# Message loop of a four-layer graph network: the older tile's product matmuls stand ahead of the next tile's source matmuls on TensorE

## The chip, the cores and the metric

The kernel runs on one core of a Trainium2 chip. The metric is the device time in microseconds, median of three runs. The profile is one further execution of the same program on the chip, taken by the hardware profiler.

## The reference

2708 nodes with 128 features each and a sparse adjacency matrix (about 8 edges in a row of 2708, each row divided by its count) go through four layers. Each layer normalises the rows, takes a relu and adds its result to x. The change concerns layer 1 and the product of layer 2 that is made beside it:

```python
# layer 1
s = node_feats @ msg_w[:, :D].T
d = node_feats @ msg_w[:, D:].T
messages = gelu(s[:, None, :] + d[None, :, :] + msg_b)
aggregated = einsum('ijd,ij->id', messages, adj)
combined = concatenate([node_feats, aggregated], axis=-1)
h = gelu(combined @ upd_w.T + upd_b) + node_feats
x = x + (h - mean(h)) / sqrt(var(h) + LN_EPS) * ln_w + ln_b
# layer 2
h = relu(layernorm(x))
x = x + relu(adj @ (h @ w2))
```

Layer 0 is a hyperbolic layer with one product by adj, layer 3 has one more product by adj, and neither is touched.

## The kernel before, in words

The 2708 rows are 22 tiles of 128 (the last has 20 rows). In a first stage (to about 222 us) the kernel reads adj transposed, keeps a mask of its nonzeros in 8-bit floats, finds for every row the columns of its edges, and runs layer 0. It also writes the rows d to a table in HBM (`d_hbm`).

Layer 1 is the message loop (L1734 to L1876). It makes the messages of existing edges only. For each tile t, `messages` (L1749) does this:

- GpSimd (POOL) issues seven indirect gathers from `d_hbm` (L1727): four into `g` (edges 3 to 6 of each row) and three into `gt` (the remaining edges, 384 to a tile). The last tile has two, both into `gt`. Each of the two buffers exists four times. The first two edges of each row, `early`, have been gathered before the loop.
- `sources(t)` (L1734 to L1747): for `gt` the s of the row that an edge belongs to is needed. Nine matmuls of TensorE (three chunks of 128 edges, three bf16 parts of s each) write it to a PSUM tile `msg`. Two such PSUM tiles exist (the other six banks hold the running product), and the matmuls `own` of the prelude use the same two.
- VectorE (DVE) adds s to `early` and `g` (L1773) and `msg` to `gt` (L1776); ScalarE (ACT) takes the gelus (L1781, L1782).
- TensorE sums the messages by row into a free part of the same `msg` tile: six matmuls on `early` and `g` (L1787) and three on `gt` with a 0/1 matrix `rt` (L1789), which the profile counts as 12 and 6, two passes each.
- ACT copies the sums to `aggs` (L1801), TensorE multiplies them by the update weights into `msg` (L1803), DVE reads that (L1804), ACT takes the gelu (L1807), and DVE adds h (L1808).

After every two tiles `update` (L1814) normalises them: DVE forms the mean (L1613), ACT squares (L1616), DVE makes a root out of nine small operations (L1604, L770 to L779, L1620), ACT scales (L1819), DVE multiplies and adds to x (L1826, L1829). The same follows for x (`jx`, `nmx`), then ACT takes the relu (L1626) and makes, with DVE (L1631, L1633), three bf16 parts of layer 2's h in `parts`. These parts go over the parts of s, which `sources` of that tile has used up.

Layer 2's product adj @ h runs in the same loop. `add_products(accs, parts, s)` (L1641) has 18 matmuls for a tile s: three parts by six blocks of columns, 512 columns each but the last (148). In tile t of the loop it takes s = t - 4 (`LAG`), called `share`, where 4 <= t < 20. The shares 16 to 19 follow after the loop (L1874 to L1876), and those of tiles 20 and 21 are in the next stage.

In 9 of the tiles from 5 to 16 DVE also compares a row tile of adj with the row's value (L1661, two halves of 1354 columns), which SyncE's queue loads. For the first tiles a prelude (L1700) makes v and tmp for four later tiles at a time.

The order on each engine is set by a scheduler that is part of the language. `queue_behind(ins)` (L763) adds one condition: what is issued inside it stands behind `ins` in its own engine's list. In `messages` these conditions give TensorE's order: the sums of tile t, then the sources of t + 1 (behind the last sum, `done`), then the product share, then the update matmul of tile t, and the sums of tile t + 1 behind that one (`sum_after`). Apart from such conditions and the data, the scheduler orders DVE and ACT itself, so their lists can differ where only TensorE's conditions do.

Of the kernel before, what the change touches and what calls it, by code (L numbers as in the profile page):

```python
# [543 lines left out]
@with_exitstack  # L544
def gnn_stack_kernel(ctx: ExitStack, tc: tile.TileContext, *args: bass.AP):
    nc = tc.nc
    N = args[0].shape[0]
    flag = ctx.enter_context(tc.tile_pool(name="flag", bufs=1)).tile([1, 1], I32, name="flag")
    with ExitStack() as sparse:
        sparse_stack(sparse, tc, flag, *args)  # L550
    failed = nc.values_load(flag[0:1, 0:1], min_val=0, max_val=1)
    with tc.If(failed > 0):
        with ExitStack() as dense:
            dense_stack(dense, tc, *args)


def sparse_stack(
# [21 lines left out]
    nc = tc.nc  # L579
    N = x_in.shape[0]  # L580
    T = -(-N // P)
# [6 lines left out]
    def rows(t):  # L588
        return min(P, N - t * P)
# [5 lines left out]
    def chunks(t):  # L595

        return NQ if rows(t) == P else tails(t) + 1
# [3 lines left out]
    def cols(t0, t1):  # L601
        return slice(t0 * P, min(t1 * P, N))
# [160 lines left out]
    def queue_behind(ins):  # L763
        return ExitStack() if ins is None else tc.issue_after(ins.ins)
# [31 lines left out]
    with ExitStack() as st:  # L796
# [142 lines left out]
        latest = {}  # L939
# [700 lines left out]
    def add_products(accs, parts, t, which=None):  # L1640

        for k in range(3):
            for b in range(len(blocks)) if which is None else which:
                sl = cols(*blocks[b])
                last = nc.tensor.matmul(  # L1645
                    accs[b][:, : sl.stop - sl.start],
                    parts[:, t, k, :],
                    mask[:, t, sl],
                    start=(t == 0 and k == 0),
                    stop=(t == T - 1 and k == 2),  # L1650
                )
        return last
# [41 lines left out]
    with ExitStack() as st_m:  # L1694
# [30 lines left out]
        def gather(g, table, n):  # L1725
            for q in range(g.shape[1]):
                nc.gpsimd.indirect_dma_start(  # L1727
                    out=g[:n, q, :],
                    out_offset=None,
                    in_=d_hbm,  # L1730
                    in_offset=bass.IndirectOffsetOnAxis(ap=table[:n, q : q + 1], axis=0),
                )

        def sources(t, after):  # L1734

            ps = ps_one.tile([P, BANK], F32, tag="one", name=f"msg{t}")
            for q in range(chunks(t)):
                for k in range(3):
                    with queue_behind(after):
                        nc.tensor.matmul(  # L1740
                            ps[:, q * D : (q + 1) * D],
                            r_all[:, t, q * P : (q + 1) * P],
                            parts[:, t, k, :],
                            start=(k == 0),
                            stop=(k == 2),
                        )
            return ps  # L1747

        def messages(t, ps, u, total, add_after, sum_after, share):  # L1749


            n = rows(t)
            nq = chunks(t)
            own_places = n == P
            if own_places:
                ge = early_d[t // EACH][:, t % EACH, :, :]
                g = gath_p.tile([P, HEAD - EARLY, D], F32, tag="g", name=f"g{t}")
                gather(g, head_c[:, t, :], n)
            gt = gath_p.tile([P, nq, D], F32, tag="gt", name=f"gt{t}")
            gather(gt, tail_c[:, t, :], P)  # L1760
            rt = hot_p.tile([P, nq, P], F32, tag="rt", name=f"rt{t}")
            with queue_behind(first):
                nc.vector.tensor_tensor(
                    rt,
                    col_i.unsqueeze(1).to_broadcast([P, nq, P]),
                    tail_r[:, t, :nq].unsqueeze(2).to_broadcast([P, nq, P]),
                    ALU.is_equal,
                )

            ahead = rows_done[t - 2] if t >= 2 else (None, None)  # L1770
            with queue_behind(add_after), queue_behind(ahead[0]):
                for a in (ge, g) if own_places else ():
                    nc.vector.tensor_add(  # L1773
                        a, a, v[:, t, :].unsqueeze(1).to_broadcast([P, a.shape[1], D])
                    )
                last = nc.vector.tensor_add(  # L1776
                    gt, gt, ps[:, : nq * D].rearrange("p (q d) -> p q d", d=D)
                )
            with queue_behind(ahead[1]):
                for a in (ge, g) if own_places else ():  # L1780
                    nc.scalar.activation(a, a, AF.Gelu)  # L1781
                nc.scalar.activation(gt, gt, AF.Gelu)  # L1782
            sums = ps[:, NQ * D : NQ * D + P]
            with queue_behind(sum_after):
                for q in range(HEAD if own_places else 0):
                    part = ge[:, q, :] if q < EARLY else g[:, q - EARLY, :]
                    nc.tensor.matmul(sums, part, ident, start=(q == 0), stop=False)  # L1787
                for q in range(nq):
                    done = nc.tensor.matmul(  # L1789
                        sums,  # L1790
                        gt[:, q, :],
                        rt[:, q, :],
                        start=(not own_places and q == 0),
                        stop=(q == nq - 1),
                    )
            next_ps = sources(t + 1, done) if t + 1 < T else None
            if share is not None:
                with queue_behind(done):
                    done = add_products(accs, parts, share)
            agg = small.tile([P, P], F32, tag="agg", name=f"aggs{t}")  # L1800
            nc.scalar.copy(agg, sums)  # L1801
            with queue_behind(done):
                new = nc.tensor.matmul(ps[:, :D], agg, upd_w[:, 1, :], start=True, stop=True)  # L1803
            nc.vector.scalar_tensor_tensor(  # L1804
                u, ps[:, :D], val[:, t : t + 1], tmp[:, t, :], op0=ALU.mult, op1=ALU.add
            )
            curved = nc.scalar.activation(u, u, AF.Gelu)  # L1807
            added = nc.vector.scalar_tensor_tensor(  # L1808
                u, u, 1.0, h[:, t, :], op0=ALU.mult, op1=ALU.add, accum_out=total
            )  # L1810
            rows_done.append((added, curved))
            return last, next_ps, new
# [31 lines left out]
        first = prelude(0)  # L1844
        begun = 1
        ps = sources(0, None)

        last_two = max(0, T - 2)
        starts = list(range(0, last_two, 2)) + list(range(last_two, T))
        for t0, t1 in zip(starts, starts[1:] + [T]):  # L1850
            n = t1 - t0
            u = small.tile([P, n, D], F32, tag="u", name=f"u{t0}")
            total = group_p.tile([P, n], F32, tag="total", name=f"totu{t0}")
            for k in range(n):
                t = t0 + k

                share = t - LAG if LAG <= t < T - 2 else None
                last, ps, new = messages(
                    t, ps, u[:, k, :], total[:, k : k + 1], last_check, new, share
                )  # L1860
                if begun < len(groups):
                    prelude(begun)
                    begun += 1
                elif t % 4 != 3 and t < T - 5 and unchecked:

                    with queue_behind(last):
                        last_check = compare(
                            unchecked.pop(0),
                            lambda k: hT[:, k * middle : (k + 1) * middle],
                            junk_p,  # L1870
                            [(0, middle), (middle, N)],
                        )
            update(t0, n, u, total)
# [183 lines left out]
```

## Time and profile before

| what | us |
|---|---|
| median of 3 runs (lowest 555.25, highest 558.63) | 555.48 |
| the profiled execution | 556.43 |
| its span | 554.6 |
| PE busy | 422.5 (76%) |
| DVE busy | 419.9 (76%) |
| ACT busy | 236.6 (43%) |
| POOL busy | 234.7 (42%) |
| mean granted TensorE clock | 0.892 of full speed |

The message loop lies between 222 and 423 us of the span. A view by stage gives busy time there: in 361.5 to 413.4 (51.9 us) PE 41.92, DVE 36.05, ACT 23.79, POOL 39.64; in 413.4 to 423.4 (10 us) PE 5.28, DVE 5.50, ACT 5.34, POOL 0.00; in 423.4 to 442.0 (18.6 us) PE 18.60, DVE 11.34.

How such lines are read: a group or a piece of the timeline begins with start and length in us, then engine, line and operation, out<-in with shapes, and how many instructions it merges. The bracket holds the idle time of the engine just before, and what ended it. A line of the waits view has the waiting engine and line, what it waited for, and the total in us, the number of waits and the longest. Waits of POOL of 0.3 us are the time between two issues and no real waits. PE matmuls overlap, so a piece of the timeline can end after the next begins.

### The profile page before, as it was taken

How to read it: one execution, taken by the hardware profiler on the slowest of the kernel's cores; microseconds unless marked ns; L12 is line 12 of the kernel's file. 1: busy time of each engine (PE TensorE's matmuls, PEld its weight loads, DVE VectorE, ACT ScalarE, POOL GpSimd, SP SyncE). 2: the span in 40 equal slices, each digit the busy share in tenths (PEclk: the TensorE clock that was granted, in tenths of full speed). 3: DMA queues.
4: the chain of work that ended last, by engine and by line, in shares of the span. 5: the costliest groups of instructions: out<-in, count | busy, mean ns of one | idle time of the engine just before them, and what ended most of it. 6: DMA issues, size and time to landing. Idle time of an engine off the chain costs nothing.

```text
span 554.6 us, 8223 instructions
## 1 busy us (share of the span) xinstructions
PE 422.5 (76%) x2504; PEld 262.1 (47%) x2504; DVE 419.9 (76%) x1743; ACT 236.6 (43%) x570; POOL 234.7 (42%) x268
## 2 busy tenths in 40 slices
PE   0981999999993062276877968879877999989994
PEld 0760354464753051265646644646553555445652
DVE  6977986767998989437679786879546599998742
ACT  2867966766424131324535434454534344300100
POOL 8800022220047777777777777777760000000000
PEclk9996899999998555668888987989997999999998
DMA  8893779970031132123146473752220250399011
GB/s 260 278 318 124 227 248 331 305 210 2 1 115 43 52 96 52 48 52 104 51 151 203 153 206 101 232 170 52 54 47 2 83 219 1 116 390 394 20 57 51
DMA packets 39332, 77.89 MB, mean 140 GB/s; under 512 B 5754, under 2 KB 18614, under 8 KB 37722
## 3 DMA queue, kind: packets, MB, share of 16 engines
q1 hardware_dynamic: 30270, 63.15, 33.1%
q0 software_dynamic: 7264, 13.40, 9.6%
q10 hardware_dynamic: 1744, 0.72, 0.5%
q8 instruction: 22, 0.36, 0.3%
q14 instruction: 32, 0.26, 0.1%
HBM read 73.63 MB, written 3.62 MB: 139 GB/s over the span
## 4 chain that ended last, share of the span: by engine, by line
PE 37%; DVE 31%; DMA 12%; POOL 6%; issue 6%; ACT 5%; ACTq 0%; DVEq 0%
PE three L1645 8%; PE acc L1324 8%; PE two L1645 7%; DMA gt<-d_hbm,tail_c 5%; DMA a<-in_adj_t_dram 4%; POOL g L1727 4%; DVE eq L1661 3%; POOL gt L1727 3%; PE msg L1787 3%; DMA layer_w<-in_L_gnn_layer_dram 2%; PE d L948 1%; DMA hT<-in_adj_dram 1%; PE pk L1028 1%; DVE mask L994 1%; PE neigh L1684 1%
## 5 line engine op out<-in xcount | busy, mean ns | idle before, releaser
L1645 PEld LDWEIGHTS <-parts 128*128 128x128 bf16 x792 | 75.3, 101 | 90.4 <-issue 9.5
L1645 PE MATMUL two<-mask,parts 128*128 128x512 fp8e4 (+1 forms) x396 | 88.8, 381 | 9.3 <-ACT parts L1630 5.1
L1727 POOL DMA_INDIRECT g<-d_hbm,head_c x84 | 82.9, 986 | 25.8 <-issue 22.6
L1324 PE MATMUL acc<-mask,parts 128*128 128x512 fp8e4 (+1 forms) x396 | 79.6, 355 | 0.7 <-DVE parts L786 0.4
L1645 PE MATMUL three<-mask,parts 128*128 128x512 fp8e4 (+1 forms) x396 | 79.0, 354 | 0.6 <-ACT parts L1630 0.5
L1727 POOL DMA_INDIRECT gt<-d_hbm,tail_c x65 | 62.7, 964 | 19.8 <-issue 15.2
L1120 POOL DMA_INDIRECT val<-in_adj_dram,ai x22 | 22.0, 998 | 104.5 <-DVE left L1108 91.3
L1324 PEld LDWEIGHTS <-parts 128*128 128x128 bf16 x396 | 36.6, 98 | 47.6 <-ACT parts L783 7.5
L1523 POOL DMA_INDIRECT early<-d_early,early_c x42 | 43.0, 1023 | 12.8 <-issue 11.9
L999 ACT ACTIVATE mask<-a 128x2048 fp8e4<-128x2048 uint32 (+3 forms) x27 | 38.2, 1434 | 10.0 <-DMA a<-in_adj_t_dram 9.8
L1661 DVE TENSOR_SCALAR_CACHE_REDUCE eq<-row,val 128x2708 fp8e4<-128x2708 f32 (+1 forms) x13 | 39.4, 3031 | 2.4 <-DMA row<-in_adj_dram 2.3
L1028 PE MATMUL pk<-mask,shifts 128*128 128x512 fp8e4 (+1 forms) x132 | 31.1, 372 | 13.0 <-ACT mask L999 12.4
L1740 PE MATMUL msg<-parts,r_all 128*128 128x128 bf16 x195 | 15.7, 227 | 19.0 <-DVE u L1804 13.7
L1661 DVE TENSOR_SCALAR_CACHE_REDUCE eq<-hT,val 128x1354 fp8e4<-128x1354 f32 x18 | 29.1, 1619 | 0.1
L1787 PE MATMUL msg<-ident,early 128*128 128x128 f32 x84 | 16.4, 327 | 16.6 <-DVE gt L1776 13.3
L1776 DVE TENSOR_TENSOR gt<-gt,msg 128x384 f32<-128x384 f32 (+1 forms) x22 | 12.0, 545 | 21.5 <-DMA gt<-d_hbm,tail_c 19.1
L1710 PE MATMUL own<-pair_w,hT 128*128 128x256 f32 x44 | 15.9, 503 | 13.6 <-ACT exs L1268 9.6
L1787 PE MATMUL msg<-ident,g 128*128 128x128 f32 x168 | 25.5, 302 | 0.0
L926 ACT ACTIVATE h<-x,n_nb,n_rstd 128x128 f32<-128x128 f32 x44 | 18.2, 486 | 17.0 <-DVE n_nb L920 17.0
L1787 PEld LDWEIGHTS msg<-ident,g 128*128 128x128 f32 x168 | 24.2, 221 | 0.2
L1740 PEld LDWEIGHTS <-r_all 128*128 128x128 fp8e4 x195 | 13.5, 102 | 22.1 <-issue 18.0
L1773 DVE TENSOR_TENSOR g<-g,v 128x512 f32<-128x512 f32 x21 | 14.5, 689 | 11.3 <-DMA g<-d_hbm,head_c 11.3
(407 smaller groups left out, 867.2 us busy)
## 6 DMA issues: line engine op xcount, KB each, us to landing
a<-in_adj_t_dram SPq DMA_DIRECT2D x25, 1024.0 KB, 7.6
row<-in_adj_dram SPq DMA_DIRECT2D x12, 1354.0 KB, 9.6
hT<-in_adj_dram SPq DMA_DIRECT2D x18, 677.0 KB, 4.1
a<-in_adj_t_dram SPq DMA_DIRECT2D x5, 296.0 KB, 4.9
g<-d_hbm,head_c POOLq DMA_INDIRECT x84
a<-in_adj_t_dram SPq DMA_DIRECT2D x5, 256.0 KB
d_hbm<-v SPq DMA_DIRECT2D x5, 256.0 KB, 3.7
out_dram<-x SPq DMA_DIRECT2D x5, 256.0 KB
```

The source lines that it names most:

```text
L926: nc.scalar.activation(h[:, t, :], x[:, t, :], AF.Relu, bias=node("nb")[:, t : t + 1], scale=node("rstd")[:, t : t + 1],)
L999: nc.scalar.activation(mask[:, g : g + n, sl], bits[:, :n, :w], AF.Sign, saturate=False)
L1028: nc.tensor.matmul(pk[:, :w], shifts[:, t, :], mask[:, t, sl], start=(t == 0), stop=(t == T - 1))
L1120: nc.gpsimd.indirect_dma_start(out=val[:, t : t + 1], out_offset=None, in_=flat, in_offset=bass.IndirectOffsetOnAxis(ap=ai[:, t : t + 1], ...
L1324: last = nc.tensor.matmul(acc[:, :w], parts[:, t, k, :], mask[:, t, sl], start=(t == 0 and k == 0), stop=(t == T - 1 and k == 2),)
L1523: nc.gpsimd.indirect_dma_start(out=early_d[t // EACH][:n, t % EACH, k, :], out_offset=None, in_=d_early, in_offset=bass.IndirectOffsetOnAx ...
L1645: last = nc.tensor.matmul(accs[b][:, : sl.stop - sl.start], parts[:, t, k, :], mask[:, t, sl], start=(t == 0 and k == 0), stop=(t == T - 1 ...
L1661: last = nc.vector.tensor_scalar(eq[:n, : c1 - c0], a, val[:n, t : t + 1], None, op0=ALU.is_equal, op1=ALU.add, accum_out=same[:n, t, k : ...
L1710: nc.tensor.matmul(ps[:, k, :, :], hT[:, (t + k) * P : (t + k + 1) * P], pair_w[:, 0::2, :], start=True, stop=True,)
L1727: nc.gpsimd.indirect_dma_start(out=g[:n, q, :], out_offset=None, in_=d_hbm, in_offset=bass.IndirectOffsetOnAxis(ap=table[:n, q : q + 1], a ...
L1740: nc.tensor.matmul(ps[:, q * D : (q + 1) * D], r_all[:, t, q * P : (q + 1) * P], parts[:, t, k, :], start=(k == 0), stop=(k == 2),)
L1787: nc.tensor.matmul(sums, part, ident, start=(q == 0), stop=False)
```

## The change

In `messages`, the call `sources(t + 1, done)` moves behind the product share. Since `done` is then the last matmul of the share where there is one, the sources stand behind it. The update matmul of tile t, which stood behind the share, now stands behind the last source matmul where there are sources. `latest` only remembers that matmul. In the lists of the two builds PE's order per tile goes from sums(t), sources(t+1), share, update(t) to sums(t), share, sources(t+1), update(t). Where there is no share (t below 4, t = 20 and 21) only the condition on the update matmul changes, and with it the scheduler's order. No instruction is added or taken away. The lists of POOL and SyncE are the same in both builds; those of DVE and ACT have the same instructions in another order. From L1734 on the changed kernel's line numbers are two higher.

```diff
+        latest = {}
+
         def sources(t, after):
 
             ps = ps_one.tile([P, BANK], F32, tag="one", name=f"msg{t}")
             for q in range(chunks(t)):
                 for k in range(3):
                     with queue_behind(after):
-                        nc.tensor.matmul(
+                        latest["source"] = nc.tensor.matmul(
                             ps[:, q * D : (q + 1) * D],
                             r_all[:, t, q * P : (q + 1) * P],
                             parts[:, t, k, :],
...
-            next_ps = sources(t + 1, done) if t + 1 < T else None
             if share is not None:
                 with queue_behind(done):
                     done = add_products(accs, parts, share)
+            next_ps = sources(t + 1, done) if t + 1 < T else None
             agg = small.tile([P, P], F32, tag="agg", name=f"aggs{t}")
             nc.scalar.copy(agg, sums)
-            with queue_behind(done):
+            with queue_behind(latest["source"] if next_ps is not None else done):
                 new = nc.tensor.matmul(ps[:, :D], agg, upd_w[:, 1, :], start=True, stop=True)
```

An example from DVE's list around tile 18. Before: small steps of the x update mixed with the add to `gt` of tile 18, then L1631, L1804 of tile 17, L1633. After: all small steps of the x update, L1631, the add to `gt` of tile 18, L1633, L1804 of tile 17.

## The prediction

> Tiles are numbered t = 0 to 21. For tile t, src(t) is its nine source matmuls, gtadd(t) the vector add that takes them out of PSUM (L1776), ega(t) the 15 summing matmuls (early, g, gt), P(s) the 18 matmuls that add tile s to the product (share s = t-4), agg(t) the update matmul (L1803), u(t) the vector operation that reads it (L1804).
>
> **What bounds the kernel now.** I first read the slices and the chain on the page: the message loop lies at about 222 to 423 us, and in it no one engine is full. The chain's long entries there are gathers and their landings. So next came the view of the gather line, which gives counts and what POOL waited for:
>
> ```profile
> L1727 POOL DMA_INDIRECT g<-d_hbm,head_c x84: 943/947/1389, 222.7 to 405.9; - x84
> L1727 POOL DMA_INDIRECT gt<-d_hbm,tail_c x65: 943/947/1263, 227.9 to 412.4; - x65
> ...
>   issue: 37.8, 124
> ```
>
> 149 gathers; 37.8/124 = 0.30 us in front of each, and the waits view of POOL has no entry longer than 0.5 us. POOL never waits for a buffer: it issues without a break from 222.7 to 412.4+0.95 = 413.3. That is 190.6/149 = 1.28 us each, seven to a tile, 8.95 us per tile (0.947+0.30 would give 8.73). Nothing on PE moves this. What PE does can only matter where it falls so far behind that POOL lacks a buffer (four per kind), or after the last gathers. The waits of PE and DVE over 222 to 424 us (total, times, longest):
>
> ```profile
> PE msg L1740 <- DVE u L1804: 13.7, 9, 2.8
> PE msg L1787 <- DVE gt L1776: 13.3, 5, 8.1
> PE two L1645 <- ACT parts L1630: 5.1, 5, 2.9
> ...
> DVE gt L1776 <- DMA gt<-d_hbm,tail_c: 19.1, 10, 3.1
> ```
>
> First line: src(t+1) stands at the head of PE and waits for u(t-1), whose read frees its PSUM tile; P, which needs nothing from it, stands behind. Second line: ega(t) starts only after gtadd(t) has read the same PSUM tile. Fourth: gtadd waits for a landing in ten of 22 tiles, tiles 18 (put down to PE, but its gathers land then), 19 and 20 among them. So at the end of the loop the gathers set the pace, and PE has caught up. Then comes the end, PE first, then DVE:
>
> ```profile
> 412.34 0.43 PE L1803 MATMUL msg<-pair_w,aggs 128*128 128x128 f32 x2
> 414.03 0.71 PE L1787 MATMUL msg<-ident,early 128*128 128x128 f32 x4 [1.27 <-DVE gt L1776]
> ...
> 415.48 0.83 PE L1789 MATMUL msg<-rt,gt 128*128 128x128 f32 x6
> 417.85 0.49 PE L1740 MATMUL msg<-parts,r_all 128*128 128x128 bf16 x6 [1.54 <-DVE u L1804]
> 419.96 0.49 PE L1803 MATMUL msg<-pair_w,aggs 128*128 128x128 f32 x2 [1.61 <-ACT aggs L1801]
> 421.02 1.22 PE L1789 MATMUL msg<-rt,gt 128*128 128x128 f32 x4 [0.58 <-ACT gt L1782]
> 422.60 0.80 PE L1803 MATMUL msg<-pair_w,aggs 128*128 128x128 f32 x2 [0.35 <-ACT aggs L1801]
> ```
>
> ```profile
> 413.43 0.55 DVE L1776 TENSOR_TENSOR gt<-gt,msg 128x384 f32<-128x384 f32 x1 [2.62 <-DMA gt<-d_hbm,tail_c]
> ...
> 414.67 0.16 DVE L1620 TENSOR_TENSOR nmx<-nmx,rx 128x2 f32<-128x2 f32 x1
> 416.22 0.43 DVE L1631 TENSOR_TENSOR leftx<-h,parts 128x256 f32<-128x256 f32 x1 [1.38 <-ACT parts L1630]
> 417.11 0.43 DVE L1633 TENSOR_TENSOR parts<-leftx,parts 128x256 bf16<-128x256 f32 x1 [0.47 <-ACT parts L1632]
> 417.45 0.35 DVE L1804 SCALAR_TENSOR_TENSOR u<-msg,val,tmp 128x128 f32<-128x128 f32 x1
> ```
>
> agg(19) is done at 412.8, but u(19) runs at 417.45, as the update of tiles 16 and 17 stands ahead of it on DVE. src(21), u(19)'s gelu and squares, the copy of the sums of tile 20 behind these on ACT (419.66), agg(20) and tile 21 all follow from it. The last 84 product matmuls start at 423.4. They and the chain of updates of tiles 18 to 21 end this stage, and PE is busy nearly throughout from there to the end.
>
> [...] the last gather of tile 20 starts at 409.88, and its add at 413.43. [...] The trace has gathers of up to 1.39 us beside 0.947, without a stated cause. [...] in this loop the granted clock is 0.62 in the first 27 us and 0.88 to 0.97 later.
>
> **The change part by part.** No instruction is added or removed; POOL's and SP's lists are the same in both builds, so no DMA moves. On PE before: ega(t), src(t+1), P(t-4), agg(t). After: ega(t), P(t-4), src(t+1), agg(t).
>
> (a) *The wait of src for u goes.* P now stands first and needs 3.5 us (399.70 to 403.17), more than the longest wait, 2.8. It frees up to 13.7 us on PE, which I cost at nothing: the gathers hide it.
>
> (b) *A wait comes in.* gtadd(t+1) needs src(t+1), and ega(t+1) needs gtadd(t+1). Before, P and agg lay between, 3.47 + 0.43 = 3.9 us. Now only agg does, 0.43. PE's round from gtadd to gtadd becomes serial: add and release 0.6, ega 2.1 (395.69 to 397.8), P 3.47, src with its release 0.7; 6.9 us at full clock. 6.9 is under 8.95, so the cover is the gather pace, with 2.0 us to spare per tile. Without it each tile would cost these 6.9 against 6.25 before (298.5, 304.7 and so on in the trace).
>
> (c) *DVE's list is reordered by the scheduler.* It now has the update's chain before gtadd and u(t) right behind it: "chain, left, gtadd(18), parts, u(17)" against "gtadd(18), chain, left, u(17)". Queued behind a gtadd that waits for src are u, the adds of the next early and g tiles, and the update chain. So I walked the new list with durations from DVE's timeline: 0.195 for each of nine small chain steps, 1.55 from nmx to left, 1.11 from nmu to L1826, 0.89 from left to parts, 0.47 for gtadd and rt, 0.94 for early and g, 1.55 for each of two compares. From gtadd to gtadd: 8.5, 7.8, 8.8, 8.9 from tile 6 to 10 (three of four tiles carry a compare); 7.8, 7.5, 7.8, 8.5, 8.8 to tile 15; 7.5, 7.8, 7.5, 7.1, 7.1 to tile 20. I start with gtadd(5) at 280.7 instead of 278.56 (it now stands behind P(0)) and gtadd(6) at 293 (before: 294.33). This gives gtadd(10) at 327, landing 325.6; gtadd(12) at 342.4, landed by 344.6. From there DVE is faster than the gathers: gtadd(20) again waits for the landing at 413.4. Without that cover the walk's own mean, 111.4/14 = 8.0 us per tile, would be the pace.
>
> (d) *Buffers of the gathers.* g of tile t+4 needs ega(t). POOL starts it some 24 us after the data of tile t have landed, and the lag I find is at most 7 us. Nothing.
>
> (e) *The end.* u(19) now stands directly behind gtadd(20): 413.9 instead of 417.45. agg(19), behind src(20), comes at about 411 against 412.34, so it isn't late. src(21) can go when ega(20) ends, 416.3 instead of 417.85. On ACT the gelu of u(19) and two squares end at 416.25; the copy of tile 20's sums runs at 416.5 instead of 419.66; gtadd(21) at 416.8 instead of 420.10. From there to the last product matmuls is as before, 3.2 to 3.3 us: they start at 420.1 instead of 423.4. The chain of tiles 18 and 19 starts at 416.2 instead of 419.79. Both move by 3.2 to 3.6 us; what is late next is the landing of tile 20 itself.
>
> The sum: 0 + 0 + 0 + 0 - 3.2. The profiled execution took 556.4 (span 554.6), so 553.2 against itself; the median of the runs is 0.95 lower, 555.48, which gives 552.3.
>
> **Rivals.**
> *Nothing gained, 555.5.* gtadd(20) now stands behind left and parts, which my walk has done at 413.0 with the landing at 413.4. If the walk is short by 0.2 us per tile from tile 12 on and DVE arrives 3 us late, the gain is gone. Against it: gathers gain about 7 us over DVE from tile 12 to 20.
> *Slower, 560.* The serial round of (b) decides once it exceeds 8.95 us. PE's share of it is 6.2 us at full clock; src took 1.12 instead of 0.66 at half clock at 322, and P 5.3 instead of 3.6 at 369. A round wholly at half clock is near 12 us. At a mean of 9.5 over tiles 6 to 20, 15 x 0.55 = 8 us are lost, less the 3.2. For it: half-clock stretches do occur in this loop. Against: 0.88 to 0.97 means rounds of 7.1 to 7.7.
> *Faster, 549.* Gathers took 4.4 us more than 149 x 1.25 = 186.2. [...] The trace doesn't show the cause.
>
> **How the numbers follow.** Forecast 0.58, by itself 550.5 to 554; nothing gained 0.17; slower 0.14, most of it over 561; faster 0.11, most of it under 549.9. 1% (5.6 us) is about what a measurement of this kernel can tell from no change. So: faster 0.10, same 0.80, slower 0.10. The range, 549.5 to 557.5, leaves out about 0.08 below and 0.12 above; it takes in the first two cases whole.
>
> **What would show it.** Right: gathers still without a break, ending near 413; no wait of src for u; waits of L1787 for gtadd in more tiles; u(19) within 1 us of gtadd(20); the 84 matmuls starting near 420. Wrong: POOL waiting for ega; gtadd(18) to gtadd(20) later than 395.1, 403.7 and 413.4; or the product matmuls starting at 423 or later although u(19) is early.

## The result and the profile after

The changed kernel takes 553.15 us (median of 10 runs, 550.89 to 556.45). The kernel before takes 557.07 in the 10 runs that belong with it (555.25 to 558.63), 1.6 us more than in the three runs that the forecast started from. The ratio is 0.9935, 95% interval 0.9906 to 0.9964: a gain of 2.0 to 5.2 us, 3.9 by the medians. The forecast step was -3.2 us. This is less than the 1% that the prediction took for about what can be told from no change, but the interval doesn't reach 1: a small gain is there.

The profiled execution has a span of 552.0 us (before: 554.6), with the same mean granted clock, 0.892. The view of the gather line comes first again (columns after the count: shortest, median and longest in ns, then first and last start). The last gather of all is the second one of tile 21:

```profile
L1727 POOL DMA_INDIRECT gt<-d_hbm,tail_c x65: 940/944/1352, 227.2 to 412.5; - x65
```

The last gather starts at 412.5, before at 412.4. So over the 190 us of loop almost nothing was gained or lost, though much moved underneath. The waits view over 222 to 424 us (total, times, longest):

```profile
PE msg L1789 <- DVE gt L1778: 29.4, 15, 7.8
...
DVE g L1775 <- DMA g<-d_hbm,head_c: 15.2, 7, 3.9
...
DVE gt L1778 <- DMA gt<-d_hbm,tail_c: 7.4, 4, 3.1
```

The 13.7 us of sources waiting for `u` have gone from the list. In their place the sums wait for gtadd 29.4 us in 15 tiles, 13.3 in 5 before. The waits for landings have partly moved from gtadd (19.1 before) to the add to `g` (11.3 before). The end of the loop, TensorE's timeline first:

```profile
411.82 0.66 PE L1742 MATMUL msg<-parts,r_all 128*128 128x128 bf16 x9
412.32 0.44 PE L1805 MATMUL msg<-pair_w,aggs 128*128 128x128 f32 x2
414.89 0.71 PE L1789 MATMUL msg<-ident,early 128*128 128x128 f32 x4 [2.13 <-DVE gt L1778]
415.44 1.75 PE L1789 MATMUL msg<-ident,g 128*128 128x128 f32 x8
416.97 1.49 PE L1791 MATMUL msg<-rt,gt 128*128 128x128 f32 x6
418.25 0.85 PE L1742 MATMUL msg<-parts,r_all 128*128 128x128 bf16 x6
...
421.45 2.88 PE L1645 MATMUL two<-mask,parts 128*128 128x512 fp8e4 x14
```

In before the same product matmuls started 1.74 us later:

```profile
423.19 3.32 PE L1645 MATMUL two<-mask,parts 128*128 128x512 fp8e4 x8
```

VectorE in after:

```profile
409.30 0.69 DVE L1775 TENSOR_TENSOR g<-g,v 128x512 f32<-128x512 f32 x1 [1.23 <-DMA g<-d_hbm,head_c]
...
411.51 0.16 DVE L1620 TENSOR_TENSOR nmx<-nmx,rx 128x2 f32<-128x2 f32 x1
413.05 0.43 DVE L1631 TENSOR_TENSOR leftx<-h,parts 128x256 f32<-128x256 f32 x1 [1.38 <-ACT parts L1630]
413.95 0.43 DVE L1633 TENSOR_TENSOR parts<-leftx,parts 128x256 bf16<-128x256 f32 x1 [0.47 <-ACT parts L1632]
414.29 0.55 DVE L1778 TENSOR_TENSOR gt<-gt,msg 128x384 f32<-128x384 f32 x1
414.75 0.35 DVE L1806 SCALAR_TENSOR_TENSOR u<-msg,val,tmp 128x128 f32<-128x128 f32 x1
```

u(19) now follows gtadd(20) at once; before, the chain nmx, left, parts lay between the two and u(19) came at 417.45. No bracket stands at gtadd(20): it doesn't wait for its data, it is queued behind the chain, and that behind the add to `g`, which waited 1.23 us for its landing. The sums of tile 20 (from 414.89) take 3.4 us, where the same 18 matmuls took 2.3 in before. The view of the windows shows why (us, then busy time of PE, PEld, DVE, ACT and POOL, then PE's granted clock, the DMA share and GB/s):

```profile
412.21:415.63 3.42, 1.29 (x13) 1.10 (x11) 1.58 (x4) 1.90 (x5) 0.96 (x2) 1.00 0.25 48
415.63:419.04 3.41, 3.41 (x21) 3.35 (x21) 1.57 (x11) 1.25 (x5) 0.00 (x0) 0.50 0.00 0
```

From 415.63 to 419.04 TensorE was granted half its clock (0.50 in the view). Before, such a stretch lay later and was twice as long, over the steps of tile 21 and the first of the last product matmuls:

```profile
417.41:420.82 3.41, 0.98 (x8) 0.61 (x7) 2.40 (x16) 1.71 (x7) 0.00 (x0) 1.00 0.00 0
420.82:427.65 6.83, 6.27 (x18) 3.14 (x19) 4.39 (x35) 2.99 (x12) 0.00 (x0) 0.50 0.01 4
```

The last product matmuls start at 421.45 (before 423.19). From there to the end of the span are 130.6 us (before 131.4). So of the 2.5 us between the spans (554.57 and 552.03) 1.7 arise before that point and 0.8 after it.

### The profile page after: what moved, and what is told of

Same layout as the page of the kernel before. It is cut to its first block, busy times and chain, and to the rows that moved or that the text cites. A ratio compares the mean times of both kernels' runs of the same rounds, so it can differ in the third digit from the quotient of the medians.

```text
span 552.0 us, 8233 instructions
## 1 busy us (share of the span) xinstructions
PE 420.9 (76%) x2504; PEld 266.1 (48%) x2504; DVE 422.0 (76%) x1743; ACT 239.5 (43%) x570; POOL 237.2 (43%) x268
## 4 chain that ended last, share of the span: by engine, by line
DVE 34%; PE 32%; issue 9%; POOL 8%; ACT 8%; DMA 7%; ACTq 0%; DVEq 0%; SPq 0%
PE three L1645 8%; PE acc L1324 6%; POOL g L1727 4%; PE two L1645 3%; POOL gt L1727 3%; DVE eq L1661 3%; PE msg L1789 2%; DMA a<-in_adj_t_dram 2%; PE pk L1028 2%; DMA layer_w<-in_L_gnn_layer_dram 2%; DMA g<-d_hbm,head_c 1%; PE u L1458 1%; PE d L948 1%; PE msg L1791 1%; ACT h L1626 1%
## 5 line engine op out<-in xcount | busy, mean ns | idle before, releaser
L1645 PE MATMUL two<-mask,parts 128*128 128x512 fp8e4 (+1 forms) x396 | 82.0, 361 | 3.3 <-ACT parts L1630 3.1
L1523 POOL DMA_INDIRECT early<-d_early,early_c x42 | 43.0, 1023 | 12.8 <-issue 11.6
L1789 PE MATMUL msg<-ident,early 128*128 128x128 f32 x84 | 17.0, 333 | 39.7 <-DVE gt L1778 29.4
L1789 PEld LDWEIGHTS msg<-ident,early 128*128 128x128 f32 x84 | 13.2, 222 | 43.5 <-DVE gt L1778 21.9
L1789 PE MATMUL msg<-ident,g 128*128 128x128 f32 x168 | 27.8, 318 | 0.0
L1789 PEld LDWEIGHTS msg<-ident,g 128*128 128x128 f32 x168 | 26.1, 233 | 0.3
L1791 PE MATMUL msg<-rt,gt 128*128 128x128 f32 x130 | 22.1, 317 | 0.7 <-ACT gt L1784 0.7
L936 PE MATMUL hTpm<-ident,h 128*128 128x128 f32 x22 | 5.6, 350 | 21.7 <-ACT h L926 21.7
```

Source lines behind the costliest of these rows:

```text
L1523: nc.gpsimd.indirect_dma_start(out=early_d[t // EACH][:n, t % EACH, k, :], out_offset=None, in_=d_early, in_offset=bass.IndirectOffsetOnAx ...
L1645: last = nc.tensor.matmul(accs[b][:, : sl.stop - sl.start], parts[:, t, k, :], mask[:, t, sl], start=(t == 0 and k == 0), stop=(t == T - 1 ...
L1791: done = nc.tensor.matmul(sums, gt[:, q, :], rt[:, q, :], start=(not own_places and q == 0), stop=(q == nq - 1),)
```

## The experiments

The theory: the gain comes from the end of the loop alone, where u(19) no longer stands behind the update chain on VectorE, and nothing done to TensorE's order before that moves the time while the gathers set the pace. The rivals: the waits of the sources that have gone are worth something all along the loop (then the order in tiles 0 to 15 gains); or the added serial round costs time that something else gives back. Ratios below are to the kernel before on the same chip (two medians of 27 runs each, 557.50 and 557.61). "Lag" is the start of the last product matmuls less the start of the last gather, which is tile 21's, in the one profiled execution of each kernel: 10.80 us before, 8.92 after.

### The new order in the first 16 tiles only, and from tile 16 on only

The diff is that of the first kernel against after; the second has `t >= 16` in its first line.

```diff
+            new_order = t < 16
+            next_ps = None
+            if t + 1 < T and not new_order:
+                next_ps = sources(t + 1, done)
             if share is not None:
                 with queue_behind(done):
                     done = add_products(accs, parts, share)
-            next_ps = sources(t + 1, done) if t + 1 < T else None
+            if t + 1 < T and new_order:
+                next_ps = sources(t + 1, done)
...
-            with queue_behind(latest["source"] if next_ps is not None else done):
+            with queue_behind(latest["source"] if new_order and next_ps is not None else done):
```

> New PE order for tiles 0 to 15, old order from tile 16 on; DVE's list at the end of the loop is then that of before (the add to gt of tile 20 amid the x update's small steps, u of tile 19 behind the parts). If the gain is made at the end of the loop, by u(19) standing directly behind the add to gt of tile 20: no gain, ratio to before 0.998 to 1.003, u(19) some 4 us behind that add, product matmuls from about 423 us. If the gain comes from the loop itself (the share covering the wait of the sources for u): ratio about 0.994 here as well.

> Old PE order for tiles 0 to 15, new order from tile 16 on. End-of-loop theory: all of the gain, ratio about 0.993 to 0.996, product matmuls from about 421 us. Loop theory: at most a quarter of it, ratio 0.998 or more.

Measured: the first 16 tiles alone 556.38 us (22 runs), ratio 0.9975 (0.9963 to 0.9986), lag 10.80, to the digit that of before. The tail alone 553.94 (6 runs), ratio 0.9923 (0.9894 to 0.9953), lag 8.91, almost that of after. VectorE's timeline of the first kernel has the old picture, a gtadd(20) that waits for its landing and a u(19) 4 us later:

```profile
413.54 0.56 DVE L1778 TENSOR_TENSOR gt<-gt,msg 128x384 f32<-128x384 f32 x1 [2.55 <-DMA gt<-d_hbm,tail_c]
...
417.57 0.35 DVE L1811 SCALAR_TENSOR_TENSOR u<-msg,val,tmp 128x128 f32<-128x128 f32 x1
```

The second has the new picture. Here gtadd(20) waits for src(20), whose matmuls start only at 414.39, after a half-clock stretch from 407.6 to 411.0 on the sums of tile 19 (8 of them in 1.92 us for 1.06):

```profile
415.09 0.56 DVE L1778 TENSOR_TENSOR gt<-gt,msg 128x384 f32<-128x384 f32 x1 [1.18 <-PE msg L1742]
415.56 0.35 DVE L1811 SCALAR_TENSOR_TENSOR u<-msg,val,tmp 128x128 f32<-128x128 f32 x1
```

So the tail by itself has a gain like that of the whole change. The first 16 tiles give 0.8 to 2.1 us (the expectation allowed no more than 0.2%); that isn't nothing, and their lag doesn't show where it comes from. It stays open.

### VectorE's list alone, with TensorE's order of before

One condition on the kernel before: gtadd(20) stands behind the last step (L1633) of the update of tiles 16 and 17. TensorE's and POOL's lists are those of before. On VectorE gtadd(20) moves, and a few small operations right behind it change places; on ScalarE the gelu of this add moves with it, behind the relu and the two casts of the update.

```diff
-                last = nc.vector.tensor_add(
-                    gt, gt, ps[:, : nq * D].rearrange("p (q d) -> p q d", d=D)
-                )
+                with queue_behind(updated[-2] if t == last_two else None):
+                    last = nc.vector.tensor_add(
+                        gt, gt, ps[:, : nq * D].rearrange("p (q d) -> p q d", d=D)
+                    )
...
-            relu_parts(parts, sl, *normal(x[:, sl, :], total, f"x{t0}"), f"x{t0}")
+            return relu_parts(parts, sl, *normal(x[:, sl, :], total, f"x{t0}"), f"x{t0}")
...
-            update(t0, n, u, total)
+            updated.append(update(t0, n, u, total))
```

> PE's order of before, untouched; one condition more on DVE: the add to gt of tile 20 stands behind the parts (L1633) of the update of tiles 16 and 17, as in the changed kernel's list, and u(19) follows it. End-of-loop theory: the order of PE isn't needed for the gain, only DVE's list at tile 20 is; ratio about 0.993 to 0.996, u(19) within 1 us of the add. Loop theory, or a theory that PE's own order makes the gain: ratio 0.998 or more.

Measured: 552.73 us (6 runs), ratio 0.9918 (0.9886 to 0.9950), lag 8.09. VectorE's timeline:

```profile
408.42 0.16 DVE L1613 TENSOR_SCALAR nmx<-totx 128x2 f32<-128x2 f32 x1
...
409.44 0.68 DVE L1773 TENSOR_TENSOR g<-g,v 128x512 f32<-128x512 f32 x1
...
411.93 0.16 DVE L1620 TENSOR_TENSOR nmx<-nmx,rx 128x2 f32<-128x2 f32 x1
413.47 0.42 DVE L1631 TENSOR_TENSOR leftx<-h,parts 128x256 f32<-128x256 f32 x1 [1.38 <-ACT parts L1630]
414.37 0.43 DVE L1633 TENSOR_TENSOR parts<-leftx,parts 128x256 bf16<-128x256 f32 x1 [0.47 <-ACT parts L1632]
414.71 0.55 DVE L1777 TENSOR_TENSOR gt<-gt,msg 128x384 f32<-128x384 f32 x1
415.17 0.35 DVE L1805 SCALAR_TENSOR_TENSOR u<-msg,val,tmp 128x128 f32<-128x128 f32 x1
```

gtadd(20) even comes 1.3 us later than before, and still the loop ends earlier, since u(19) comes 2.3 us earlier. TensorE's new order is not needed for a gain of this size. In the change, what it did at the end of the loop was to bring the scheduler to another list on VectorE. Gelu and add moved together here, so this kernel doesn't separate VectorE's list from ScalarE's.

### The add to g(20) behind the root

In after, gtadd(20) came 0.86 us later than before because the update chain stood behind an add that waited for a landing. Here, on after, the add to `g` of tile 20 stands behind the last small step (L1620) of that chain.

```diff
-        nc.vector.tensor_mul(nm, nm, r)
+        latest["form"] = nc.vector.tensor_mul(nm, nm, r)
...
-                    nc.vector.tensor_add(
-                        a, a, v[:, t, :].unsqueeze(1).to_broadcast([P, a.shape[1], D])
-                    )
+                    with queue_behind(formed_at[-2] if a is g and t == last_two else None):
+                        nc.vector.tensor_add(
+                            a, a, v[:, t, :].unsqueeze(1).to_broadcast([P, a.shape[1], D])
+                        )
...
             update(t0, n, u, total)
+            formed_at.append(latest["form"])
```

> The changed kernel, with the add to g of tile 20 behind the last small step (L1620) of the x update of tiles 16 and 17. In the changed kernel's trace that add waited 1.23 us for its gathers (409.3) with the update's steps queued behind it, and the add to gt of tile 20 came at 414.29 behind them. If this is what took 1 us of the forecast gain: add to gt of tile 20 near 413.3, product matmuls about 1 us earlier than in the changed kernel (420.5), ratio to before 0.991 to 0.995. If the late add has another cause (DVE late for itself): no difference to the changed kernel.

Measured: 552.41 us (6 runs), ratio 0.9906 (0.9880 to 0.9933), lag 6.99. VectorE's timeline (its last gather started at 409.99, so the times lie 2.5 us earlier than in after):

```profile
403.50 0.55 DVE L1779 TENSOR_TENSOR gt<-gt,msg 128x384 f32<-128x384 f32 x1
403.96 0.16 DVE L1613 TENSOR_SCALAR nmx<-totx 128x2 f32<-128x2 f32 x1
...
407.72 0.69 DVE L1776 TENSOR_TENSOR g<-g,v 128x512 f32<-128x512 f32 x1
...
411.03 0.56 DVE L1779 TENSOR_TENSOR gt<-gt,msg 128x384 f32<-128x384 f32 x1 [0.24 <-DMA gt<-d_hbm,tail_c]
411.50 0.35 DVE L1807 SCALAR_TENSOR_TENSOR u<-msg,val,tmp 128x128 f32<-128x128 f32 x1
```

The chain is done in time and gtadd(20) waits for its landing again. It starts 3.54 us after the last gather of its own tile (407.49) and 1.04 after the last gather of all, as in before. The lag is 1.93 us shorter than in after, where about 1 was expected: 0.72 is the earlier gtadd(20), and 1.21 is that the sums and sources behind it ran at full clock in this execution. It is the lowest median of all kernels with the layer's output, though its interval overlaps that of after, so that it is faster than after isn't shown.

### The same two conditions with TensorE's order of before

> PE's order of before, and two conditions on DVE's list at tile 20 only: the add to g behind the last small step of the x update of tiles 16 and 17, the add to gt behind their parts. By the end-of-loop theory this has the gain of the changed kernel with the late add mended: time from the last gather's issue to the first of the last product matmuls 7.0 us (10.8 before, 8.9 in the changed kernel), ratio to before 0.989 to 0.994, the same as the changed kernel with that one condition. If PE's new order adds something of its own: slower than that kernel by 1 us or more in this stretch.

The edit is the two diffs above, both on the kernel before. Measured: 555.95 us (22 runs), ratio 0.9974 (0.9955 to 0.9994), lag 9.66 instead of the 7.0 expected. A miss. VectorE's timeline:

```profile
404.92 0.56 DVE L1778 TENSOR_TENSOR gt<-gt,msg 128x384 f32<-128x384 f32 x1 [2.38 <-DMA gt<-d_hbm,tail_c]
...
409.57 0.21 DVE L1613 TENSOR_SCALAR nmx<-totx 128x2 f32<-128x2 f32 x1
...
412.72 0.16 DVE L1620 TENSOR_TENSOR nmx<-nmx,rx 128x2 f32<-128x2 f32 x1
412.90 0.69 DVE L1774 TENSOR_TENSOR g<-g,v 128x512 f32<-128x512 f32 x1
414.64 0.43 DVE L1631 TENSOR_TENSOR leftx<-h,parts 128x256 f32<-128x256 f32 x1 [1.05 <-ACT parts L1630]
...
415.88 0.55 DVE L1778 TENSOR_TENSOR gt<-gt,msg 128x384 f32<-128x384 f32 x1
```

With the old order gtadd(19), which waits for its landing, stands ahead of the root of the u update, so x's chain begins (L1613) 4.65 us after gtadd(19), against 0.46 in the kernel with the new order. It ends too late, and gtadd(20), bound behind it, comes 2.55 us after the last gather's start instead of 1.04. In this respect the list that goes with TensorE's new order is the better one.

A late chain doesn't make the first condition worthless, though. The kernel with that condition alone has the same late chain (408.42, 4.50 us after its gtadd(19)) and is the faster one. On VectorE and ScalarE these two kernels differ in a single thing, the later place of the add to `g` of tile 20 and of its gelu. With the old order that add did not wait (409.44, no bracket), so there was nothing to win by moving it. It costs something instead: the gelu of `g` now comes between the relu and the cast of the chain on ScalarE, and from the end of the root (L1620) to `left` (L1631) it takes 1.92 us instead of 1.54. This is 0.4 of the 1.6 us by which the lags differ. The rest is a half-clock stretch from 417.3 to 420.7, in which the sums of tile 20 ran (8 of them in 1.70 us for 1.06). The medians differ by 3.2 us, and the intervals don't overlap; how much of that is the move, and how much the clock, is not shown.

How much of each lag is lowered clock can be estimated by comparing the same steps at full clock: from gtadd(20) to gtadd(21) 3.64 us, from there to the product matmuls 2.31, and 2.11 from the first sum of tile 19 to its share (all three from the kernel with the later add to `g`: 411.03 to 414.67 to 416.98, and 404.10 to 406.21).

| kernel | ratio to before | lag, us | of it lowered clock (estimate) |
|---|---|---|---|
| before | 1 | 10.80 | 0.8 |
| after | 0.9935 | 8.92 | 1.2 |
| new order in tiles 0 to 15 | 0.9975 | 10.80 | 0.8 |
| new order from tile 16 | 0.9923 | 8.91 | 1.5 |
| old order, gtadd(20) bound | 0.9918 | 8.09 | 0 |
| new order, add to `g` bound | 0.9906 | 6.99 | 0 |
| old order, both bound | 0.9974 | 9.66 | 1.2 |

Without the lowered clock, the estimate leaves 10.0 us where u(19) stands behind the chain (before and the first 16 tiles), and 7.0 to 8.5 in the five kernels where it follows gtadd(20) at once. The medians gain 0.5 to 2.1 us more than the lags of the single executions have shrunk. The profiled executions also differ by up to 3 us in where the gathers begin and in what follows the lag (130.6 to 133.6 us), so this remainder is not assigned to a cause.

### Without the cover: three gathers a tile in place of seven

Both kernels here leave out the gathers into `g` of tiles 0 to 20; fixed tiles, set to zero once, take their place, so that the output isn't the layer's. All other work stays.

```diff
-                g = gath_p.tile([P, HEAD - EARLY, D], F32, tag="g", name=f"g{t}")
-                gather(g, head_c[:, t, :], n)
+                g = fixed[t % 4]
```

> Leaves out the four gathers into g of tiles 0 to 20 (four fixed tiles, set to zero once, take their place), so that the output isn't the layer's; all work of PE, DVE and ACT stays, in the order of before. POOL needs three gathers, some 3.8 us per tile, and no longer covers PE and DVE. Theory (the gathers set the pace of the loop, and the order of PE before is the quicker one without them): the adds to gt of tiles 6 to 20 take 14 x 7.0 to 7.5 us = 98 to 105 us instead of 119, with waits of the sources for u still there. Rival (DVE or PE sets the pace already): the same 119 us.

> The same left out (gathers into g replaced by fixed tiles, output not the layer's), in the order of the changed kernel. Theory: the serial round and DVE's list (walked at 8.0 us per tile in the prediction) show once the gathers no longer cover them: tiles 6 to 20 take 108 to 112 us, 0.3 to 0.7 us per tile more than with the old order, less the 3 us at the end; so about 2 to 7 us slower than the old order without g gathers. Rival (the share in front of the sources takes waits off PE that cost time): faster than the old order here too, by up to 13 us.

Measured: 523.03 us with the order of before (4 runs, ratio 0.9385, 0.9343 to 0.9428) and 530.72 with the new one (4 runs, ratio 0.9519, 0.9476 to 0.9561). From gtadd(6) to gtadd(20) it is 105.5 us with the old order, 7.5 a tile, and 114.0 with the new one, 8.15 a tile. Each is a little above its expected range, but the direction is the expected one. POOL now waits for buffers (in the kernel with the old order 40.0 us in 8 waits, which the view puts down to the copies of the sums), so the engines set the pace, and the new order is 7.7 us slower. TensorE's lists are those of before and after; VectorE's and ScalarE's differ from them in some places, since the scheduler chose anew. TensorE's timeline of the kernel with the new order:

```profile
342.85 0.68 PE L1788 MATMUL msg<-ident,early 128*128 128x128 f32 x4 [1.92 <-DVE gt L1777]
...
344.93 3.63 PE L1645 MATMUL two<-mask,parts 128*128 128x512 fp8e4 x18
348.40 0.66 PE L1742 MATMUL msg<-parts,r_all 128*128 128x128 bf16 x9
348.90 0.44 PE L1804 MATMUL msg<-pair_w,aggs 128*128 128x128 f32 x2
351.68 1.20 PE L1788 MATMUL msg<-ident,early 128*128 128x128 f32 x4 [2.34 <-DVE gt L1777]
```

And VectorE's of the same kernel:

```profile
348.97 0.16 DVE L1604 TENSOR_SCALAR au<-ssqu 128x2 f32<-128x2 f32 x1
...
350.80 0.16 DVE L1620 TENSOR_TENSOR nmu<-nmu,ru 128x2 f32<-128x2 f32 x1
350.97 0.56 DVE L1777 TENSOR_TENSOR gt<-gt,msg 128x384 f32<-128x384 f32 x1
```

TensorE's round from 342.85 is done at 349.3, the sources at 349.06. gtadd could run then, but VectorE has only just begun the root's chain (348.97), after two halves of a compare and four other operations, and comes to gtadd at 350.97, without any wait. TensorE stands still for 2.34 us. In the old order the 18 product matmuls stand at this place; that they would have filled the gap is argued, not shown. Over 270 to 385 us TensorE so waits for gtadd 14.6 us in 11 tiles, and gtadd waits for the sources 0.4 us once.

So the pace here looks like that of VectorE's list, with TensorE tied to it, rather than that of TensorE's serial round of 6.9 by itself. The prediction's walk through VectorE's list supports this tile by tile. Of the 14 intervals from gtadd(6) to gtadd(20) in this kernel 12 lie within 0.4 us of what the walk had. The other two are 0.8 and 1.4 us longer, and each has a half-clock stretch in it (310.7 to 314.1 and 351.6 to 355.0; the first four sums in each took 1.20 us, in the round from 368.44 at full clock 0.68); a third stretch (276.5 to 279.9) left its interval as the walk had it.

### The share split around the sources

On the kernel just shown: a third of the product share ahead of the sources, two thirds behind them.

```diff
-                    done = add_products(accs, parts, share)
+                    done = add_products(accs, parts, share, ks=[0])
             next_ps = sources(t + 1, done) if t + 1 < T else None
+            if share is not None:
+                with queue_behind(latest["source"]):
+                    done = add_products(accs, parts, share, ks=[1, 2])
...
-            with queue_behind(latest["source"] if next_ps is not None else done):
+            with queue_behind(latest["source"] if next_ps is not None and share is None else done):
```

> The same left out (gathers into g replaced by fixed tiles, output not the layer's). PE's order: sums, first third of the share (6 matmuls), sources of the next tile, the other 12, update. The first third covers part of the wait for u, the other two thirds the add to gt. If the serial round of PE is what costs time in the changed order: faster than both, by 2 us or more against the old order. If DVE's list sets the pace in all three: within 2 us of the old order.

Measured: 529.92 us (4 runs, ratio 0.9516, 0.9466 to 0.9566), 113.8 us from gtadd(6) to gtadd(20): within 1 us of the unsplit one, and 6.9 us slower than the old order. Neither branch of the expectation came true: matmuls behind the sources did not mend it, and the three kernels do not lie within 2 us. The waits view of this kernel over 222 to 396 us says what came instead:

```profile
PE two L1645 <- ACT parts L1630: 11.6, 4, 5.5
...
PE msg L1788 <- DVE gt L1777: 6.6, 7, 3.9
```

The waits for gtadd have shrunk from 20.8 us to 6.6, and the product matmuls now wait 11.6 us for the parts of h, the end of the update chain (1.2 in the unsplit kernel). The scheduler had ordered VectorE anew, so this kernel changes two things. It shows that the loss isn't mended by filling this one gap on TensorE. It doesn't measure how much of the 7.7 us is VectorE's list.

## Why the prediction was right

Each letter is a part of the prediction.

(a) The wait of the sources, up to 13.7 us, was priced at nothing. That holds nearly: the last gather starts within 0.1 us of where it did, and the new order in 16 of 22 tiles brings 0.8 to 2.1 us, whose place is open.

(b) The serial round of 6.9 us and its cover. In after, one round at full clock runs from 406.24 (first sum of tile 19) to 412.48 (end of src(20)), 6.24; with the add's 0.6 that is 6.84. The gather pace was again 190.5/149 = 1.28 us each. The cover was real: without it the new order costs 7.7 us. The price named for that case, "6.9 against 6.25", would have given 14 x 0.65 = 9.1 us from gtadd(6) to gtadd(20). Measured are 8.5, which is near for the wrong reason, since the kernels then ran at 8.15 and 7.5 a tile and not at these numbers. The prediction named two paces for the new order, 6.9 here and 8.0 in (c); the slower one decides.

(c) The walk through VectorE's list gave 8.0 us a tile as its pace without cover; measured without it, 8.15. In after itself it gave gtadd(6) 293, gtadd(10) 327 and gtadd(12) 342.4; measured 293.91, 328.76 and 344.49. What it missed is the end, where it let gtadd(20) wait for the landing again. In after gtadd(18), gtadd(19) and gtadd(20) come at 396.43, 405.63 and 414.29, without a wait of their own and later than the 395.1, 403.7 and 413.4 that the prediction had named as a sign of being wrong. The wait for a landing had moved to the add to `g` (1.23 us for tile 20), and the update chain was queued behind that. So this sign did show. It cost 0.9 us and not the gain, because the gain needs only u(19) right behind gtadd(20).

(d) Buffers: POOL has no wait over 0.5 us in after. Holds.

(e) The end, "-3.2", measured -1.74: the last product matmuls start at 421.45 against 423.19 (the prediction took 423.4 for the latter). u(19) came at 414.75 instead of 413.9, from the miss in (c): +0.85. agg(19) came at 412.32, no earlier than before and not "at about 411", which held nothing up. The sums of tile 20 took 3.4 us instead of 2.3, as the half-clock stretch now fell on them: +1.1. So src(21) began at 418.25 instead of 416.3, and the chain of tiles 18 and 19 at 417.40 instead of 416.2 (before 419.79). From gtadd(21) to the product matmuls it was 2.3 us (419.14 to 421.45) instead of the 3.3 carried over from before, as these steps now ran at full clock. So the product matmuls start at 421.45 against 420.1 forecast. The 0.8 us by which the rest of the span is shorter stood in no step of the sum. It can't be put down to the vanished half-clock stretch, since two other kernels without one there took 132.3 us for this rest, more than before's 131.4. One execution makes 2.5 us in all; the medians say 3.9 (2.0 to 5.2). So the place and the mechanism were right. The close agreement of 0.65% with the forecast 0.6% is partly luck: the traced step at the end was about half of the forecast one, and the rest of the measured gain came from where the sum had nothing. The term missing from the sum was the place of the lowered clock, about 1 us each way.

The rivals: "nothing gained" named the right weak point, a gtadd(20) late behind left and parts. It was late by 0.9 us, not by the 3 that it needed. "Slower" needed a round over 8.95 us. Single intervals got there (the longest from tile 6 on were 10.1 and 9.9 us, one behind a late landing, one in a stretch from 371 to 378 us with a granted clock of 0.50), but not the mean: gtadd(6) to gtadd(20) took 120.4 us, before 119.1. "Faster" from other gather durations: not seen, 1.28 us each in both.

## What to carry to other kernels

When an engine off the critical path is reordered, look first at the lists of the other engines: here the moved matmuls were worth at most 2.1 us over the first 16 tiles, and most of the gain came because the scheduler no longer put a chain with two round trips through ScalarE between gtadd(20) and one small operation that the end of the loop waits for. One condition at that place did the same. A second condition, which shortened the lag in one list, lengthened it in the other, so ask first whether the operation to be moved waits at all. Before calling a loss hidden, take the cover away in an experiment: it showed that this order costs 7.7 us with three gathers a tile in place of seven.

## What the hardware showed that was not expected

The stretch of lowered clock near the end of the loop stands at another place from kernel to kernel: 420.8 to 427.6 before and 415.6 to 419.0 after, both with a granted clock of 0.50, 407.6 to 411.0 with the new order from tile 16, none from 400 to 430 in the kernels with one condition on gtadd(20) or with the later add to `g`. The idle time of TensorE ahead of the sums of tile 20 was 2.13 us in after and 2.35 in the kernel with one condition, so the length of this gap by itself doesn't decide it.

Nor does the busy time of TensorE over some 3.4 us by itself. It was 0.98 us (29%) from 417.41 in before and 1.29 us (38%) from 412.21 in after, and in both the granted clock was 0.50 in what followed. In the kernel with one condition it was 1.04 us (31%) from 412.00, and the clock stayed at 1.00:

```profile
412.00:415.40 3.40, 1.04 (x7) 0.59 (x5) 1.55 (x5) 1.80 (x5) 1.20 (x2) 1.00 0.25 51
415.40:418.80 3.40, 3.01 (x26) 2.63 (x26) 2.10 (x15) 1.76 (x8) 0.00 (x0) 1.00 0.00 0
```

What decides it is left open. Each kernel has one profiled execution, so it isn't shown either whether the stretch comes and goes at this place without any change of the kernel. On the sums and sources at the end of the loop it is worth about 1.2 us in after (the estimate in the table above), more than some of the differences that this document is about.
